# Four column groups for the weighted sums of a graph attention layer, with sums by ones

## The chip, the cores and the metric

The kernel runs on one core of a Trainium2 chip. The metric is the device time of one execution in microseconds (us); lower is better. The core's engines are named as in the profile: PE (TensorE matmul) with PEld (its weight loads), DVE (VectorE), ACT (ScalarE), POOL (GpSimd) and SP (SyncE, which here only issues DMAs). Each works through its own queue in order; they wait for one another by semaphores.

## The reference, cut to what matters

The whole computation is a stack of four graph layers over x of shape 128 x 128 x 128 (samples, tokens, features) with an integer adjacency of the same shape. Each layer normalizes its input, applies a relu, and adds its result to x. The change concerns layer 2, a graph attention with four heads of 32 features, and two helpers that it shares with layer 3, an attention with one head of 128 features.

```python
h = jnp.maximum(_layernorm(x, axis=-1), 0.0)
x = x + _L2_gnn_ref(h, adj, L2_gnn_W, L2_gnn_b, L2_gnn_a)

def _L2_gnn_ref(x, adj, W, b, a):
    H, D = 4, 32
    h = (x @ W + b).reshape(Bb, Nn, H, D)
    e_i = jnp.einsum('bnhd,d->bnh', h, a[:D, 0])
    e_j = jnp.einsum('bnhd,d->bnh', h, a[D:, 0])
    e = e_i[:, :, None, :] + e_j[:, None, :, :]
    e = jnp.where(e > 0, e, 0.2 * e)
    e = jnp.where(adj[..., None] > 0, e, NEG)
    attn = jax.nn.softmax(e, axis=2)
    out = jnp.einsum('bijh,bjhd->bihd', attn, h)
    return out.reshape(Bb, Nn, H * D)
```

Layer 3 has the same form with one head, and an elu on its result.

## The kernel before, in words

The kernel has three long stages: up to about 1500 us layer 0 and the pairwise differences of layer 1; up to about 2317 us the rest of layer 1, during which the DMA engines are busy; and then the last stage, layers 2 and 3. Only the last stage is edited. Samples are worked on in 32 groups of G = 4. `attention(g)` lists the work of one group as steps; every step has a name, an engine, a cost, the steps that it follows, the PSUM tiles that it takes and those that it gives back. `_planned` takes the lists of all groups, with a distance of PERIOD = 12 us between groups, and writes out one order for all engines from those costs; that order is then issued as it stands. Several groups are under way at once, so that each engine's queue mixes steps of different groups and layers. PSUM is shared as ONE = 4 tiles of one bank (tag "one") and TWO = 2 tiles of two banks (tag "two").

The steps of one group, for layer 2:

- `off` (L1190, POOL) makes a mask of missing edges from the stored bytes. `y`, `yl`, `po`, `x1` end layer 1 and give x.
- `layer(2, ...)` begins with `moments` (L1217, L1219, DVE) and `root` (L225, L226, L1223, L1224, POOL), which give the factor `rs` and offset `nb` of each token. `normed` (L1229) applies them with a relu, one sample at a time, on ACT. `turned` (L1235, PE) transposes, a copy to `hT` (L1304, ACT) follows, and `projected` (L1241, L1244, PE) multiplies by the layer's weights. The result `pr` holds the values and, in its last columns, both score vectors.
- `scores` (L1252, DVE) takes the scores out as `v`; `values` (L1257, L1258, POOL) presets the value tile `wr` and `values2` (L1267, ACT) copies the values in. In layer 2 a head has 33 columns: 32 values and a one, so that a product with `wr` also gives the softmax's sum.
- `split` (L1283, L1285, POOL) splits the scores into bf16 pieces, `crossed` (L1290, PE) transposes them, ACT copies `left` (L1312), and `right` (L1296, DVE) spreads the other factor over four parts with 0/1 masks, for each layer once.
- For each sample k: `summed` (L1332, L1335, PE) makes the scores of all four heads in one bank and masks them, for two samples at a time; `exps` (L1318, L1319, ACT) takes two exponentials; `higher` (L1322, DVE) takes the larger one as `e`, 128 x 4 x 128 with the neighbours on the partitions.
- `weighed` (L1345, PE) multiplies: for each head, `e` of that head is the stationary operand and a window of 128 columns of `wr` is the moving one. The first 33 columns of each result are values and sum. `scaled` (L1359, L1360, DVE) takes the reciprocal of the sums of two samples (128 x 8) and multiplies; after both pairs, `x2` (L1365, DVE) adds to x.

Layer 3 then runs the same steps with one head; its products are L1381 and its division L1385 and L1386. Three DVE steps and an exponential give the elu, and SP stores the group (L1400).

Of the kernel before, what the change touches and what calls it, by code (L numbers as in the profile page):

```python
# [9 lines left out]
F32 = mybir.dt.float32  # L10
I32 = mybir.dt.int32
BF16 = mybir.dt.bfloat16
U8 = mybir.dt.uint8
AF = mybir.ActivationFunctionType
OP = mybir.AluOpType
AX = mybir.AxisListType

P = 128
G = 4
# [20 lines left out]
ONE, TWO = 4, 2  # L40
# [128 lines left out]
def tile_gnn_stack(ctx: ExitStack, tc: tile.TileContext, a: dict, out: bass.AP):  # L169
    nc = tc.nc  # L170
# [18 lines left out]
    ident = const.tile([P, P], F32, name="ident")  # L189
# [3 lines left out]
    ones = const.tile([P, P], F32, name="ones")  # L193
# [23 lines left out]
    M8 = [res.tile([P, G, P], U8, tag=f"m{g}", name=f"m{g}") for g in range(NG)]  # L217
# [44 lines left out]
    with tc.tile_pool(name="c0", bufs=1) as c0, tc.tile_pool(name="p0", bufs=2) as p0, ExitStack() as ctx0:  # L262

        both = c0.tile([P, 2, P], F32, name="both")
# [280 lines left out]
        flat = a["adj"].rearrange("b t s -> b (t s)").rearrange("b (c n) -> c b n", c=PARTS)  # L545
# [100 lines left out]
        with tc.If(nc.values_load(flag, min_val=0, max_val=1) > 0) as cmp, \  # L646
# [6 lines left out]
            for g in range(NG):  # L653
                x = pr.tile([P, G, P], F32, name="x")
# [5 lines left out]
                hT = pr.tile([P, G, P], F32, name="hT")  # L660
# [3 lines left out]
                o = pr.tile([P, G, P], F32, name="o")  # L664
# [107 lines left out]
    with tc.tile_pool(name="bn", bufs=1) as bn:  # L772


        w_all, w_last, n = 2.0 * G * (KH - 1) * P, 1.0 * G * P, 1.0 * NB * P * P
        last = bn.tile([P, 1], F32, name="last")
# [16 lines left out]
        m = fold_sum(ST1[:, :, :, 0])  # L793
# [24 lines left out]
    with tc.tile_pool(name="c1", bufs=1, reuse_waits="tile") as c1, \  # L818
# [7 lines left out]
                         start=True, stop=True)  # L826
        own = c1.tile([P, 1], F32, name="own")
# [11 lines left out]
                         start=True, stop=True)  # L839
# [7 lines left out]
        for n in range(2):  # L847
            t = c1.tile([P, G, 1 + 2 * KH], F32, name=f"sk{n}")
# [296 lines left out]
    with tc.If(nc.values_load(bounded, min_val=0, max_val=1) > 0) as cmp, \  # L1145
# [10 lines left out]
        def attention(g):  # L1156


            t, steps = {}, []

            def step(name, engine, cost, after, work, takes=(), last=()):
                steps.append(((g, name), engine, cost, [(g, n) for n in after], takes, last, work))

            def sb(name, shape, dtype=F32):
                t[name] = p3.tile(shape, dtype, tag=name, bufs=BUFS[name], name=name)
                return t[name]

            def bank(name, shape=(P, G, P), dtype=F32):
                t[name] = ps3.tile(list(shape), dtype, tag="one", bufs=ONE, name=name)
                return t[name]  # L1170

            def two(name, n):

                t[name] = ps3.tile([P, 2, 512], F32, tag="two", bufs=TWO, name=name)
                t[name] = t[name][:, :, 0:2 * n].rearrange("p a (b c) -> p a b c", b=2)
                return t[name]
# [10 lines left out]
            lx = () if on_chip else ("lx",)  # L1187

            def masked():
                nc.gpsimd.tensor_scalar(sb("off", [P, G, P], BF16), M8[g], 0.0, None, op0=OP.is_equal)  # L1190

            step("off", "Pool", 1.5, lx, masked)
            step("y", "ACT", 0.75, () if on_chip else ("lz",), lambda: nc.scalar.activation(
                t["y"], t["y"], AF.Identity, bias=bias2, scale=scale2[:, 0:1]))
            step("yl", "DVE", 0.65, ("y",), lambda: nc.vector.scalar_tensor_tensor(
# [2 lines left out]
            def rest():  # L1198
                po = bank("po")
                for k in range(G):  # L1200
# [4 lines left out]
                 last=("po",))  # L1205

            def layer(n, heads, wx, first):

                q = lambda name: name + str(n)
                N = P + 2 * heads  # L1210
                mv, rs, nb = q("mv"), q("rs"), q("nb")
# [14 lines left out]
                def normed():  # L1226
                    h = sb("h", [P, G, P])
                    for k in range(G):
                        nc.scalar.activation(h[:, k, :], t["x"][:, k, :], AF.Relu, bias=t[nb][:, k:k + 1],  # L1229
                                             scale=t[rs][:, k:k + 1])  # L1230

                def turned():
                    pt = bank(q("pt"))
# [19 lines left out]

                def values():
                    if first:
                        wr = sb(q("wr"), [P, G + 1, 4, 33])
                        nc.gpsimd.memset(wr[:, 0:G, :, 32:33], 1.0)  # L1257
                        nc.gpsimd.memset(wr[:, G, 0:3, :], 0.0)  # L1258
                    else:
                        wr = sb(q("wr"), [P, G, 129])  # L1260
                        nc.gpsimd.memset(wr[:, :, P:], 1.0)

                def values2():
                    pr, wr = t[q("pr")], t[q("wr")]
                    for a in range(2):
                        if first:
                            nc.scalar.copy(wr[:, 2 * a:2 * a + 2, :, 0:32],  # L1267
                                           pr[:, a, :, 0:P].rearrange("p b (c d) -> p b c d", c=4))
                        else:
                            nc.scalar.copy(wr[:, 2 * a:2 * a + 2, 0:P], pr[:, a, :, 0:P])  # L1270
# [22 lines left out]
                rows, own = (32 * G, own_h) if first else (32, own_k)  # L1293

                def right():
                    nc.vector.tensor_tensor(sb(q("right"), [P, 4, P], BF16)[0:rows],  # L1296
                                            t[q("pe")][0:rows, 1:2, :].to_broadcast([rows, 4, P]),
                                            own[0:rows, :, None].to_broadcast([rows, 4, P]), OP.mult)

                step(mv, "DVE", 1.05, ("x1",) if first else ("x2",), moments)  # L1300
                step(rs, "Pool", 1.7, (mv,), root)
                step(q("h"), "ACT", 1.2, (rs,), normed)
                step(q("pt"), "PE", 0.5, (q("h"),), turned, takes=(q("pt"),))
                step(q("hT"), "ACT", 0.52, (q("pt"),), lambda: nc.scalar.copy(sb(q("hT"), [P, G, P]), t[q("pt")]),  # L1304
                     last=(q("pt"),))
                step(q("pr"), "PE", 1.0, (q("hT"),), projected, takes=("2" + q("pr"),))
                step(q("v"), "DVE", 0.3, (q("pr"),), scores)
                step(q("w1"), "Pool", 0.3, (q("h"),), values)
                step(q("wr"), "ACT", 0.65, (q("v"), q("w1")), values2, last=("2" + q("pr"),))
                step(q("sp"), "Pool", 1.2, (q("v"),), split)  # L1310
                step(q("pe"), "PE", 0.2, (q("sp"),), crossed, takes=(q("pe"),))
                step(q("left"), "ACT", 0.3, (q("pe"),), lambda: nc.scalar.copy(  # L1312
                    sb(q("left"), [P, P], BF16)[0:rows], t[q("pe")][0:rows, 0, :]))
                step(q("right"), "DVE", 0.6, (q("left"),), right, last=(q("pe"),))

            def exps(ps, e):

# [7 lines left out]
            for k in range(G):  # L1325
                ps, e, pv = f"ps{k}", f"e{k}", f"pv{k // 2}"

                def summed(k=k):

                    for j in (k, k + 1):  # L1330
                        r = slice(32 * j, 32 * j + 32)
                        nc.tensor.matmul(bank(f"ps{j}"), t["left2"][r, :], t["right2"][r, :, :], start=True,  # L1332
                                         stop=False, skip_group_check=True)
                    for j in (k, k + 1):
                        nc.tensor.matmul(t[f"ps{j}"], t["off"][:, j, :], no_edge[:, None, :].to_broadcast([P, 4, P]),  # L1335
                                         start=False, stop=True, skip_group_check=True)

                def weighed(k=k, e=e, pv=pv):

                    if k % 2 == 0:  # L1340
                        t[pv] = ps3.tile([P, 2, 4, P], F32, tag="two", bufs=TWO, name=pv)
                    flat = t["wr2"].rearrange("p k c d -> p (k c d)")
                    for hd in range(4):
                        at = 33 * (4 * k + hd)
                        nc.tensor.matmul(t[pv][:, k % 2, hd, :], t[e][:, hd, :], flat[:, at:at + P],  # L1345
                                         start=True, stop=True)

                if k % 2 == 0:
                    step(ps, "PE", 0.8, ("right2", "off"), summed, takes=(ps, f"ps{k + 1}"))
                step(e, "ACT", 1.05, (f"ps{k // 2 * 2}",), lambda ps=ps, e=e: exps(ps, e))  # L1350
                step(e + "m", "DVE", 0.62, (e,), lambda ps=ps, e=e: higher(ps, e), last=(ps,))
                step(f"w{k}", "PE", 0.95, (e + "m", "wr2") + ((f"w{k - 1}",) if k % 2 else ()), weighed,
                     takes=("2" + pv,) if k % 2 == 0 else ())
                if k % 2:
                    def scaled(k=k, pv=pv):
                        sums = sb("sums2", [P, 2, 4, 1])
                        if k == 1:
                            sb("o2", [P, G, P])
                        nc.vector.reciprocal(sums, t[pv][:, :, :, 32:33])  # L1359
                        nc.vector.tensor_tensor(t["o2"][:, k - 1:k + 1, :].rearrange("p k (a b) -> p k a b", a=4),  # L1360
                                                t[pv][:, :, :, 0:32], sums.to_broadcast([P, 2, 4, 32]), OP.mult)

                    step(f"o{k}", "DVE", 0.55, (f"w{k}",) + (("o1",) if k == 3 else ()), scaled, last=("2" + pv,))

            step("x2", "DVE", 0.62, ("o3",), lambda: nc.vector.scalar_tensor_tensor(  # L1365
                t["x"], t["o2"], -1.0, t["x"], op0=OP.add, op1=OP.add))

            layer(3, 1, w3x, False)

# [40 lines left out]
    with cmp.Else(), tc.tile_pool(name="c2", bufs=1) as c2, tc.tile_pool(name="p2", bufs=5) as p2, \  # L1410
# [25 lines left out]
        left = c2.tile([3, 4], F32, name="left")  # L1436
# [188 lines left out]
```

## Time and profile before

| | us |
|---|---|
| median of three runs | 2778.75 (2771.28 to 2781.27) |
| the profiled execution's own time | 2781.11 |
| its span | 2779.3 |
| first instruction of the last stage (L1193) | 2317.6 |
| PE, DVE, ACT, POOL busy over the span | 2457.4, 2472.0, 2388.7, 1724.0 |

The span runs from the profiled execution's first to its last instruction; the execution's own time has 1.8 us more around it. Busy time counts an engine as busy while at least one of its instructions runs. Instructions of one engine overlap by a little, so that the mean length of one times the count is more than the busy time. A matmul of f32 operands appears as two passes, each with its own weight load. Shapes are partitions x elements; "out<-in" are the program's names of the tiles. "Idle before" is the time for which the engine stood idle before instructions of that group, followed by what ended the wait.

### The profile page before, as it was taken

To read this page: it belongs to the slowest core of one execution; us is meant where nothing else is said; L and a number is where in the kernel's file an instruction comes from. 1 tells how busy PE (TensorE), PEld (TensorE's weight loads), DVE (VectorE), ACT (ScalarE), POOL (GpSimd) and SP (SyncE) were. 2 spreads that over 40 slices of the span, in tenths; PEclk is the share of its full clock that TensorE was granted. 3 is DMA by queue.
4 is the path that set the end of the run, shared out by engine and by line. 5 is a ranking of instruction groups with operands and counts; after the bars stand their busy time and mean duration, and the time that the engine had idled before them with its cause. 6 is when DMAs were issued, how large, how long until landed. Compare 5 with 4: busy or idle time off the path is not lost.

```text
span 2779.3 us, 42065 instructions
## 1 busy us (share of the span) xinstructions
PE 2457.4 (88%) x14521; PEld 1182.0 (43%) x14521; DVE 2472.0 (89%) x4712; ACT 2388.7 (86%) x2837; POOL 1724.0 (62%) x1629
## 2 busy tenths in 40 slices
PE   3899999999999999999998789888888897999896
PEld 2333333333333333333332344444444445777675
DVE  4899999999999999999999688888888887899976
ACT  4899999999999999999998778778778766899985
POOL 5799999999999999999997001111000115565642
PEclk7999999999999999999999899999999999999998
DMA  7455555555555555555543899999999971121110
GB/s 283 171 223 201 212 201 210 210 212 201 208 201 208 211 209 207 208 207 215 206 193 125 330 409 411 410 411 410 409 410 410 409 266 54 46 69 58 58 31 25
DMA packets 195933, 635.66 MB, mean 229 GB/s; under 512 B 32755, under 2 KB 100470, under 8 KB 132214
## 3 DMA queue, kind: packets, MB, share of 16 engines
q1 hardware_dynamic: 195264, 632.62, 58.6%
q8 instruction: 120, 1.97, 0.3%
q14 instruction: 111, 0.91, 0.1%
q10 hardware_dynamic: 438, 0.17, 0.0%
HBM read 328.84 MB, written 303.89 MB: 228 GB/s over the span
## 4 chain that ended last, share of the span: by engine, by line
ACT 33%; PE 22%; DVE 19%; issue 11%; DMA 10%; POOL 3%; SPq 1%; ACTq 0%; DVEq 0%; POOLq 0%
ACT d L360 11%; ACT z L336 11%; PE hp L322 6%; PE ps L871 5%; DMA rows<-sk 4%; DVE d L312 3%; DMA u<-rows 3%; DVE z L914 3%; DMA z<-hp 3%; PE hp L325 2%; ACT h L1229 2%; PE pk L878 2%; PE pv L1345 2%; ACT o L462 1%; ACT h L503 1%
## 5 line engine op out<-in xcount | busy, mean ns | idle before, releaser
L312 POOL TENSOR_TENSOR d<-xe 128x2048 f32<-128x2048 f32 x256 | 1074.1, 4202 | 67.1 <-PE hp L322 48.9
L322 PE MATMUL hp<-d,w1T 128*64 128x512 f32 x4096 | 999.4, 603 | 119.8 <-ACT z L336 96.8
L360 ACT ACTIVATE d<-d 128x2048 f32<-128x2048 f32 x384 | 734.6, 1935 | 24.7 <-POOL d L312 18.2
L312 DVE TENSOR_TENSOR d<-xe,xp 128x2048 f32<-128x2048 f32 x256 | 579.5, 2264 | 5.8 <-PE hp L322 3.1
L322 PEld LDWEIGHTS hp<-d,w1T 128*64 128x64 f32 x4096 | 286.2, 137 | 640.4 <-issue 466.6
L336 ACT COPY z<-hp 128x1024 f32<-128x1024 f32 x512 | 516.9, 1028 | 47.1 <-PE hp L325 24.4
L962 POOL TENSOR_TENSOR x<-x,bt 128x512 f32<-128x512 f32 x32 | 46.5, 1455 | 672.1 <-DMA x<-x 629.0
L350 DVE BATCH_NORM_STATS2 st<-z 128x6 f32<-128x512 f32 x512 | 349.3, 682 | 42.4 <-ACT z L336 42.1
L351 DVE BATCH_NORM_STATS2 st<-z 128x6 f32<-128x512 f32 (+1 forms) x512 | 329.3, 643 | 0.0
L914 DVE SCALAR_TENSOR_TENSOR z<-z 128x2048 f32<-128x2048 f32 x128 | 296.6, 2317 | 6.5 <-ACT z L896 6.5
L896 ACT ACTIVATE z<-z,bias,scale 128x2048 f32<-128x2048 f32 x128 | 267.1, 2087 | 9.3 <-DVE bias L809 7.7
L325 PE MATMUL hp<-both_t,xw 128*64 128x512 f32 x1024 | 268.3, 596 | 0.0
L900 ACT ACTIVATE zr<-z,bias,scale 128x2048 f32<-128x2048 f32 x128 | 267.3, 2088 | 0.9 <-DMA z<-hp 0.9
L871 PE MATMUL ps<-z,w2z 128*32 128x512 f32 x1024 | 144.7, 638 | 65.1 <-DVE z L914 64.9
L878 PEld LDWEIGHTS pk<-pick,su 128*128 128x128 f32 x1024 | 127.4, 196 | 136.2 <-DVE su L892 94.0
L878 PE MATMUL pk<-pick,su 128*128 128x16 f32 x1024 | 139.9, 269 | 19.9 <-DVE su L892 19.3
L1345 PE MATMUL pv<-wr,e 128*128 128x128 f32 x1024 | 141.7, 285 | 5.8 <-DVE e L1322 4.0
L871 PE MATMUL ps<-z,w2l 128*32 128x512 f32 x1024 | 142.7, 626 | 0.0
L871 PE MATMUL ps<-zr,w2r 128*32 128x512 f32 x1024 | 141.0, 623 | 0.0
L325 PEld LDWEIGHTS hp<-both_t,xw 128*64 128x64 f32 x1024 | 80.7, 138 | 140.7 <-issue 140.7
L1345 PEld LDWEIGHTS pv<-wr,e 128*128 128x128 f32 x1024 | 129.4, 197 | 13.5 <-DVE e L1322 4.1
L1322 DVE SCALAR_TENSOR_TENSOR e<-e,ps 128x512 f32<-128x512 f32 x160 | 106.8, 677 | 25.9 <-ACT ps L1319 25.1
(243 smaller groups left out, 3823.2 us busy)
## 6 DMA issues: line engine op xcount, KB each, us to landing
hp<-z SPq DMA_DIRECT2D x248, 1024.0 KB, 3.9
z<-hp SPq DMA_DIRECT2D x248, 1024.0 KB, 14.2
x<-x SPq DMA_DIRECT2D x118, 256.0 KB, 5.9
u<-rows SPq DMA_DIRECT2D x32, 384.0 KB, 11.6
x<-in_x_dram SPq DMA_DIRECT2D x32, 256.0 KB, 3.1
adj<-in_adj_dram SPq DMA_DIRECT2D x32, 256.0 KB, 3.5
part<-in_adj_dram SPq DMA_DIRECT2D x16, 512.0 KB, 7.6
out_dram<-x SPq DMA_DIRECT2D x32, 256.0 KB, 2.4
```

The lines of the kernel that those rows point to most:

```text
L312: eng.tensor_tensor(d, ahead, x[:, None, None, :].to_broadcast([P, 2, KC, P]), OP.max if t == BY_MAX else OP.subtract)
L322: nc.tensor.matmul(hp[64 * hh:64 * hh + 64, c:c + 512], w1T2 if by_max else w1T, d[:, hh, c:c + 512], start=True, stop=not by_max, skip_gr ...
L325: nc.tensor.matmul(hp[64 * hh:64 * hh + 64, c:c + 512], XW[i // NT // 2][:, i // NT % 2, :], both_t.rearrange("p h k i -> p h (k i)")[:, h ...
L336: nc.scalar.copy(half_of(b, t), linear.pop(i))
L350: nc.vector.bn_stats(st[:, 2 * t, :], hs[:, 0:512])
L351: nc.vector.bn_stats(st[:, 2 * t + 1, :], hs[:, 512:1024 - P * last])
L360: nc.scalar.activation(diffs[i], diffs[i], AF.Abs)
L871: nc.tensor.matmul(ps[32 * c:32 * c + 32, :], w[:, w0:w0 + 32], v[:, 512 * c:512 * c + 512], start=j0 == 0, stop=w is w2r, skip_group_chec ...
L878: nc.tensor.matmul(pk[:, kk, 0:16], su[:, kk, :], pick.rearrange("p h j -> p (h j)"), start=True, stop=True)
L900: nc.scalar.activation(zr, z1, AF.Relu, bias=bias1, scale=scale1[:, 0:1])
L914: nc.vector.scalar_tensor_tensor(z0, z0, 0.01, z0, op0=OP.mult, op1=OP.max)
L1345: nc.tensor.matmul(t[pv][:, k % 2, hd, :], t[e][:, hd, :], flat[:, at:at + P], start=True, stop=True)
```

## The change

Five edits, all in the last stage:

- In `weighed`, the operands change places: the 32 value columns of a head are stationary and `e` of that head, 128 columns, is moving. Head hd writes to partitions 32·hd to 32·hd + 31, so that the four heads use four column groups of PE's array. A second set of four products has 32 columns of ones as the stationary operand and gives the sums, repeated over the 32 partitions of a head. All four samples write into one two-bank tile `pv2`, values in its first bank, sums in its second.
- `scaled` runs once for a group, after the last sample: a reciprocal of 128 x 512 and a product of 128 x 512. Its result has features on the partitions, so `by_token` transposes it on PE into `ot`, and `x2` reads `ot`. The value tile has 32 columns for a head; its presets in layer 2 go.
- `normed` moves from ACT to POOL, without the relu; the copy to `hT` does the relu. This holds for both layers.
- `right` moves from DVE, one instruction, to ACT, four instructions, each with a mask as its per-partition scale. This too holds for both layers.
- `off` becomes a multiplication by -1 and an addition of 1 in place of a comparison with zero. The costs given to the planner follow, and its order with them.

```diff
             def masked():
-                nc.gpsimd.tensor_scalar(sb("off", [P, G, P], BF16), M8[g], 0.0, None, op0=OP.is_equal)
+                nc.gpsimd.tensor_scalar(sb("off", [P, G, P], BF16), M8[g], -1.0, 1.0, op0=OP.mult, op1=OP.add)
-            step("off", "Pool", 1.5, lx, masked)
+            step("off", "Pool", 0.7, lx, masked)
...
                     for k in range(G):
-                        nc.scalar.activation(h[:, k, :], t["x"][:, k, :], AF.Relu, bias=t[nb][:, k:k + 1],
-                                             scale=t[rs][:, k:k + 1])
+                        nc.gpsimd.tensor_scalar(h[:, k, :], t["x"][:, k, :], t[rs][:, k:k + 1], t[nb][:, k:k + 1],
+                                                op0=OP.mult, op1=OP.add)
...
                     if first:
-                        wr = sb(q("wr"), [P, G + 1, 4, 33])
-                        nc.gpsimd.memset(wr[:, 0:G, :, 32:33], 1.0)
-                        nc.gpsimd.memset(wr[:, G, 0:3, :], 0.0)
+                        sb(q("wr"), [P, G, 4, 32])
...
                 def right():
-                    nc.vector.tensor_tensor(sb(q("right"), [P, 4, P], BF16)[0:rows],
-                                            t[q("pe")][0:rows, 1:2, :].to_broadcast([rows, 4, P]),
-                                            own[0:rows, :, None].to_broadcast([rows, 4, P]), OP.mult)
+                    to = sb(q("right"), [P, 4, P], BF16)
+                    for part in range(4):
+                        nc.scalar.activation(to[0:rows, part, :], t[q("pe")][0:rows, 1, :], AF.Identity,
+                                             scale=own[0:rows, part:part + 1])
...
-                step(q("h"), "ACT", 1.2, (rs,), normed)
+                step(q("h"), "Pool", 1.85, (rs,), normed)
-                step(q("hT"), "ACT", 0.52, (q("pt"),), lambda: nc.scalar.copy(sb(q("hT"), [P, G, P]), t[q("pt")]),
+                step(q("hT"), "ACT", 0.52, (q("pt"),), lambda: nc.scalar.activation(
+                    sb(q("hT"), [P, G, P]), t[q("pt")], AF.Relu),
                      last=(q("pt"),))
-                step(q("right"), "DVE", 0.6, (q("left"),), right, last=(q("pe"),))
+                step(q("right"), "ACT", 0.95, (q("left"),), right, last=(q("pe"),))
...
-                    flat = t["wr2"].rearrange("p k c d -> p (k c d)")
-                    for hd in range(4):
-                        at = 33 * (4 * k + hd)
-                        nc.tensor.matmul(t[pv][:, k % 2, hd, :], t[e][:, hd, :], flat[:, at:at + P],
-                                         start=True, stop=True)
+                    if k == 0:
+                        two("pv2", 256)
+                    for n, left in enumerate((t["wr2"][:, k], ones.rearrange("p (a b) -> p a b", a=4))):
+                        for hd in range(4):
+                            nc.tensor.matmul(t["pv2"][32 * hd:32 * hd + 32, n, k // 2, P * (k % 2):P * (k % 2 + 1)],
+                                             left[:, hd, :], t[e][:, hd, :], start=True, stop=True,
+                                             skip_group_check=True)
...
-                        nc.vector.reciprocal(sums, t[pv][:, :, :, 32:33])
-                        nc.vector.tensor_tensor(t["o2"][:, k - 1:k + 1, :].rearrange("p k (a b) -> p k a b", a=4),
-                                                t[pv][:, :, :, 0:32], sums.to_broadcast([P, 2, 4, 32]), OP.mult)
-                    step(f"o{k}", "DVE", 0.55, (f"w{k}",) + (("o1",) if k == 3 else ()), scaled, last=("2" + pv,))
-            step("x2", "DVE", 0.62, ("o3",), lambda: nc.vector.scalar_tensor_tensor(
-                t["x"], t["o2"], -1.0, t["x"], op0=OP.add, op1=OP.add))
+            def scaled():
+                sums, o = sb("sums2", [P, G, P]), sb("o2", [P, G, P])
+                both = t["pv2"].rearrange("p n a b -> p n (a b)")
+                nc.vector.reciprocal(sums.rearrange("p k c -> p (k c)"), both[:, 1, :])
+                nc.vector.tensor_tensor(o.rearrange("p k c -> p (k c)"), both[:, 0, :],
+                                        sums.rearrange("p k c -> p (k c)"), OP.mult)
+            def by_token():
+                to = bank("ot")
+                for k in range(G):
+                    nc.tensor.transpose(to[:, k, :], t["o2"][:, k, :], ident)
+            step("o2", "DVE", 1.3, ("w3",), scaled, last=("2pv2",))
+            step("ot", "PE", 0.6, ("o2",), by_token, takes=("ot",))
+            step("x2", "DVE", 0.62, ("ot",), lambda: nc.vector.scalar_tensor_tensor(
+                t["x"], t["ot"], -1.0, t["x"], op0=OP.add, op1=OP.add), last=("ot",))
```

More of the change, by code (lines that the diff above doesn't have):

```diff
@@ L1266, in values2 @@
                         if first:
-                            nc.scalar.copy(wr[:, 2 * a:2 * a + 2, :, 0:32],
+                            nc.scalar.copy(wr[:, 2 * a:2 * a + 2, :, :],
                                            pr[:, a, :, 0:P].rearrange("p b (c d) -> p b c d", c=4))
@@ L1307, in layer @@
                 step(q("v"), "DVE", 0.3, (q("pr"),), scores)
-                step(q("w1"), "Pool", 0.3, (q("h"),), values)
+                step(q("w1"), "Pool", 0.0 if first else 0.15, (q("h"),), values)
                 step(q("wr"), "ACT", 0.65, (q("v"), q("w1")), values2, last=("2" + q("pr"),))
@@ L1336, in summed, with weighed @@
                                          start=False, stop=True, skip_group_check=True)
-                def weighed(k=k, e=e, pv=pv):
-                    if k % 2 == 0:
-                        t[pv] = ps3.tile([P, 2, 4, P], F32, tag="two", bufs=TWO, name=pv)
-                    flat = t["wr2"].rearrange("p k c d -> p (k c d)")
-                    for hd in range(4):
-                        at = 33 * (4 * k + hd)
-                        nc.tensor.matmul(t[pv][:, k % 2, hd, :], t[e][:, hd, :], flat[:, at:at + P],
-                                         start=True, stop=True)
+                def weighed(k=k, e=e):
+                    if k == 0:
[5 more added lines that the diff above has]
+                                             skip_group_check=True)
                 if k % 2 == 0:
@@ L1351, in attention @@
                 step(e + "m", "DVE", 0.62, (e,), lambda ps=ps, e=e: higher(ps, e), last=(ps,))
[L1352 to L1360, printed above, removed]
-                                                t[pv][:, :, :, 0:32], sums.to_broadcast([P, 2, 4, 32]), OP.mult)
-                    step(f"o{k}", "DVE", 0.55, (f"w{k}",) + (("o1",) if k == 3 else ()), scaled, last=("2" + pv,))
-            step("x2", "DVE", 0.62, ("o3",), lambda: nc.vector.scalar_tensor_tensor(
-                t["x"], t["o2"], -1.0, t["x"], op0=OP.add, op1=OP.add))
+                step(f"w{k}", "PE", 0.6, (e + "m", "wr2") + ((f"w{k - 1}",) if k else ()), weighed,
+                     takes=("2pv2",) if k == 0 else ())
+            def scaled():
[12 more added lines that the diff above has]
+                t["x"], t["ot"], -1.0, t["x"], op0=OP.add, op1=OP.add), last=("ot",))
             layer(3, 1, w3x, False)
```

## The prediction

> **What bounds the kernel now.** I read the page's share of busy time first, then its slices, where DMA falls from nine tenths to one or two for the last seven slices: that is the stage the change touches, and nothing before it is edited. The table by windows gives that stage (first line, from its first instruction to the end) and its steady part (second line, from the fourth output store at 2415.4 us to the twenty-eighth at 2738.9 us, 24 groups of four samples). Columns: stretch, length, then busy us of each engine with its instructions.
>
> ```profile
> core 0: us, PE busy (x) PEld busy (x) DVE busy (x) ACT busy (x) POOL busy (x), PEclk, DMA share, GB/s
> 2317.00:2780.00 463.00, 402.19 (x2912) 320.69 (x2912) 381.11 (x1219) 382.62 (x896) 252.71 (x712) 0.94 0.15 45
> 2415.40:2738.90 323.50, 294.18 (x2188) 236.65 (x2187) 278.27 (x884) 280.31 (x658) 173.00 (x501) 0.97 0.17 52
> ```
>
> The steady stage costs 323.5 / 24 = 13.5 us a group. Over 32 groups the whole stage keeps PE 12.57, DVE 11.91, ACT 11.96 and POOL 7.9 us busy per group. Three engines are level and together set the pace; DVE idles 81 us of the 462 us from 2317 to the end. So an engine that is relieved brings little while the other two stay, and an engine that gets 2 us more sets the end alone. What the edits concern is in the groups kept apart by shape (count | busy us, mean ns | idle before):
>
> ```profile
> L1322 DVE SCALAR_TENSOR_TENSOR e<-e,ps 128x512 f32<-128x512 f32 x160 | 106.8, 677 | 25.9 <-ACT ps L1319 25.1
> L1360 DVE TENSOR_TENSOR o<-pv,sums 128x256 f32<-128x256 f32 x64 | 27.2, 424 | 2.2
> L1386 DVE TENSOR_TENSOR o<-pv,sums 128x512 f32<-128x512 f32 x32 | 22.1, 691 | 1.1
> L1296 DVE TENSOR_TENSOR right<-pe,own_h 128x512 bf16<-128x512 bf16 x32 | 21.6, 682 | 2.1 <-ACT left L1312 2.1
> L1296 DVE TENSOR_TENSOR right<-pe,own_k 32x512 bf16<-32x512 bf16 x32 | 21.4, 668 | 0.5 <-ACT left L1312 0.5
> L1359 DVE RECIPROCAL sums<-pv 128x8 f32<-128x8 f32 x64 | 12.6, 197 | 15.8 <-PE pv L1345 15.8
> L1252 DVE COPY v<-pr 128x16 f32<-128x16 f32 x64 | 7.7, 163 | 3.9 <-PE pr L1244 3.7
> L1252 DVE COPY v<-pr 128x4 f32<-128x4 f32 x64 | 7.2, 155 | 5.9 <-PE pr L1244 5.5 <-PE pe L1290 0.2
> L1385 DVE RECIPROCAL sums<-pv 128x4 f32<-128x4 f32 x32 | 5.4, 170 | 12.3 <-PE pv L1381 12.3
> ```
>
> The small rows matter most. A copy of 16 columns takes 8 ns more than one of 4, under 1 ns a column. A reciprocal of 8 columns takes 27 ns more than one of 4: **about 6.75 ns a column**. Today only 2 x 8 + 4 columns a group pass through it.
>
> ```profile
> L1345 PE MATMUL pv<-wr,e 128*128 128x128 f32 x1024 | 141.7, 285 | 5.8 <-DVE e L1322 4.0 <-ACT wr L1267 1.4 <-DVE o L1360 0.2
> L1229 ACT ACTIVATE h<-x,nb,rs 128x128 f32<-128x128 f32 x256 | 105.4, 491 | 26.9 <-POOL nb L1224 12.8 <-POOL wr L1261 8.0 <-DVE st L1217 4.3
> L1312 ACT COPY left<-pe 128x128 bf16<-128x128 bf16 x32 | 8.8, 282 | 2.3 <-PE pe L1290 2.3
> L1312 ACT COPY left<-pe 32x128 bf16<-32x128 bf16 x32 | 8.0, 249 | 4.3 <-PE pe L1290 4.2
> ```
>
> Here 1024 matmuls are 32 a group: each f32 product is two passes. Last, the timeline of TensorE in the stage before this one, where four column groups are already in use:
>
> ```profile
> 1898.82 0.27 PE L940 MATMUL pt<-ident,u 128*128 128x128 f32 x1
> 1899.03 1.06 PE L871 MATMUL ps<-z,w2z 128*32 128x512 f32 x8
> 1899.91 1.04 PE L871 MATMUL ps<-z,w2l 128*32 128x512 f32 x8
> ```
>
> Eight 512-column passes end in 1.06 us, two rounds of four, 0.43 us a round: the groups run at once. The step from 128-column to 32-column tiles cost 0.20 us from start to start, where transposes in a row follow each other every 0.11 us.
>
> [...]
>
> **The change, per group.**
>
> *Sums by ones.* The stationary ones repeat every softmax sum over a head's 32 rows, so the sums fill 128 x 512, and the two reciprocals of 8 columns become one of 512. On DVE two reciprocals (0.23 us from start to start) and two products (0.42, less 0.08 of overlap) go: -1.14 us. One 512-column product from PSUM comes: 0.69 - 0.08 = +0.61. The reciprocal is the unknown. From below: [...]as for L1386, 0.7 us. From the row's slope: 0.14 + 512 x 6.75 ns = 3.6. [...]I take 4.4: with 0.14 fixed it gives 173 and 207 ns for 4 and 8 columns, against 170 and 197 on average.
>
> *Right factors to ScalarE.* DVE loses two of 0.59 us pitch: -1.18 (in the timeline `right` starts at 2521.53 us and its follower at 2522.12). ACT gains eight activations, a PSUM copy of that size plus one pointer: about 375 ns, 282 ns apart: +2.26.
>
> *Norms to GpSimd.* ACT loses eight h of about 0.39 (four last 1.65 us in the timeline): -3.15, so ACT goes to 11.96 - 3.15 + 2.26 = 11.1. The relu rides on the copy of hT at no cost. POOL gains eight one-input 128x128 steps; between the 0.27 of its 128x4 steps (L225) and an estimate of 0.5 I take 0.4: +3.2. The mask as multiply and add costs 0.62 at its fastest elsewhere (median 0.94) instead of 1.53: -0.6 to -0.9. The memsets of wr save 0.3. POOL: about 10, still not the bound, even at 0.5 a step. Its two h's stand ahead of other groups' splits in its queue, so left and right come later; PE's tuned slack of several groups in flight covers that, and if not, up to 1 us a group is in my upper end.
>
> *Products.* PE drops 32 passes of 0.112 = 3.58 us. It gains, per k, four rounds of four passes of 128 columns, each round a quarter of 0.43 = 0.107, plus one mode change in and one out (0.09 each) and a weight load laid bare (0.1): 0.72, or 2.9 for four. Four transposes add 0.44. Net -0.3: PE about 12.3. From above, with no concurrency, 64 x 0.11 = 7.0.
>
> *DVE in sum*: 11.91 - 1.14 + 0.61 - 1.18 + 4.4 = **14.6 us**, 2.7 more than now and 2.3 above PE. Over 32 groups, 467 us against 381.
>
> *Waits.* Today half of the values come free after two small operations; now one two-bank tile is held from the first product until reciprocal and product are through, 5.1 us, one of the two such tiles. In the changed order of instructions PE reaches the transposes `ot` in one steady group after transposing a split, projecting values twice and transposing an h, some 2.9 us: PE then stands about 2 us, and behind `ot` are the next products and scores. On DVE itself, the scores' splits (`v`), maxima (`e`) and the moments of other groups queue behind the reciprocal; GpSimd already waited 41.3 us for `v` in 2400 to 2700 us. SP only has stores later; its loads are long done. In the tail the last group passes reciprocal, transposes and two `right` steps alone: about +5 us.
>
> *Sum.* DVE is now clearly ahead of the others, so it starves less on average, but PE's stand at `ot` and the tail give it back. I keep 75 of its 81 us idle: 467 + 75 = 542 us for the stage against 462, **+80 us**. The profiled execution took 2781.1 us (span 2779.3 and 1.8 around it), so 2861; the median of the runs, 2778.75, is 2.4 lower: 2859. With 3.6 for the reciprocal DVE's work is 441: +54, 2833. Idle between 50 and 110 us gives +55 to +115.
>
> **Rivals.**
> *The reciprocal is cheap* (0.7 us, 1.3 ns a column). Then DVE is 10.9, ACT 11.1, PE 12.3: the stage gains 0.3 to 0.9 us a group, less a longer tail: 2750 to 2775, say 2765. For it speaks only that 27 ns is a small difference of short instructions; against it, 64 and 32 of them and the copies beside them. It decides below about 1.7 us for 512 columns, where DVE comes back to 11.9.
> *PE's stand at `ot` grows*: both engines wait for each other in turn, 17.5 to 18 us a group: 2910 to 2930. Against it: several groups are in flight.
> *The column groups do not overlap at 128 columns* (the change does not do what it says): PE 12.57 + 3.4 + 0.44 = 16.4 us, DVE hidden behind it: about 2910. Against it, the lines at 1899 us.
>
> **How the numbers follow.** DVE bound by the reciprocal 0.75, growing stand 0.12, no overlap 0.05, cheap reciprocal 0.08 (of which 0.02 within 0.5%, some 14 us, about what a measurement of this kernel can tell from no change). The range 2822 to 2900 holds the main case with both its reciprocal prices and idle bounds, and the lower edge of the standing PE.
>
> **What would show it.** A row of 128x512 reciprocals at about 4.4 us (right), under 1.7 us (the main step is wrong); DVE over 90% busy in the steady part with PE and ACT under 80%; `right` near 0.37 us, h on POOL near 0.4; the first passes of four heads starting within some 10 ns of each other; PE's wait at `ot` put down to DVE's product.

## Result, and the profile after

The changed kernel takes 2851.58 us, median of four runs (2848.05 to 2852.57), against 2778.03 us for the kernel before on the same chip: 1.0268 times its time, 95% interval 1.0256 to 1.0281. The profiled execution took 2852.57 us with a span of 2850.8. The prediction was 2859. The last stage alone grew: from its first instruction to the end 461.7 us before and 536.6 after.

The table by windows of the changed kernel, whole last stage and steady part (fourth to twenty-eighth output store); columns as before, PEclk being the granted TensorE clock as a share of full speed:

```profile
core 0: us, PE busy (x) PEld busy (x) DVE busy (x) ACT busy (x) POOL busy (x), PEclk, DMA share, GB/s
2314.17:2850.80 536.63, 411.70 (x4064) 284.73 (x4064) 435.00 (x1088) 354.49 (x896) 332.44 (x902) 0.88 0.13 39
2424.20:2810.00 385.80, 304.02 (x3061) 210.50 (x3061) 321.91 (x790) 265.83 (x678) 238.60 (x656) 0.88 0.14 44
```

A group now costs 385.8 / 24 = 16.1 us. Divided by 32, the stage keeps PE 12.9, DVE 13.6, ACT 11.1 and POOL 10.4 us busy. DVE now stands at the top, 0.7 us above PE, with ACT well below. But in the steady part DVE is busy for only 83% of the time (321.91 / 385.80), PE for 79% and ACT for 69%, and PE's mean granted clock is 0.88 where it was 0.97. Both matter below.

The groups that answer to those shown of before:

```profile
L1229 POOL TENSOR_SCALAR h<-x,rs,nb 128x128 f32<-128x128 f32 x256 | 117.9, 474 | 1.4
L1358 DVE RECIPROCAL sums<-pv 128x512 f32<-128x512 f32 x32 | 107.3, 3352 | 15.7 <-PE pv L1344 15.6
L1322 DVE SCALAR_TENSOR_TENSOR e<-e,ps 128x512 f32<-128x512 f32 x160 | 105.8, 677 | 20.2 <-ACT ps L1319 19.9
...
L1344 PE MATMUL pv<-e,wr 128*32 128x128 f32 x1024 | 60.5, 305 | 17.7 <-DVE e L1322 11.9 <-DVE o L1359 2.8 <-DVE v L1252 2.4
L1344 PE MATMUL pv<-e,ones 128*32 128x128 f32 x1024 | 58.2, 296 | 0.0
...
L1244 PE MATMUL pr<-w3x,hT 128*128 128x130 f32 x256 | 42.7, 320 | 14.5 <-DVE o L1359 8.4 <-DVE v L1252 2.1 <-ACT ps L1319 1.6
...
L1296 ACT ACTIVATE right<-pe,own_h 128x128 bf16<-128x128 bf16 x128 | 36.5, 380 | 0.0
...
L1296 ACT ACTIVATE right<-pe,own_k 32x128 bf16<-32x128 bf16 x128 | 35.0, 343 | 0.0
...
L1365 PE MATMUL ot<-ident,o 128*128 128x128 f32 x128 | 26.4, 343 | 29.3 <-DVE o L1359 21.2 <-DVE sums L1389 4.0 <-ACT hT L1303 2.0
...
L1359 DVE TENSOR_TENSOR o<-pv,sums 128x512 f32<-128x512 f32 x32 | 22.1, 691 | 1.1
...
L1190 POOL TENSOR_SCALAR off<-m 128x512 bf16<-128x512 uint8 x32 | 21.7, 684 | 0.1
...
L1241 PE MATMUL pr<-b_parts,ones 3*128 3x272 bf16 x64 | 13.7, 297 | 7.0 <-DVE o L1359 6.9
```

One instruction a group, the reciprocal, takes 3.35 us and 107 us in all, as much as all 160 maxima of the scores. The row of `ot` shows PE idle for 29.3 us ahead of the new transposes, 21.2 of them until DVE's product ended. The same product ends another 18.1 us of PE's idle time, ahead of `pr` (8.4 and 6.9) and of the weighted sums (2.8): these write to two-bank tiles, and `pv2` is one of the two.

The timeline of DVE and PE of the changed kernel around one such division:

```profile
2561.50 3.35 DVE L1358 RECIPROCAL sums<-pv 128x512 f32<-128x512 f32 x1
2564.89 0.69 DVE L1359 TENSOR_TENSOR o<-pv,sums 128x512 f32<-128x512 f32 x1
...
2568.48 0.65 DVE L1322 SCALAR_TENSOR_TENSOR e<-e,ps 128x512 f32<-128x512 f32 x1
2571.81 0.26 DVE L1252 COPY v<-pr 128x16 f32<-128x16 f32 x2 [2.68 <-PE pr L1244]
2574.00 0.69 DVE L1322 SCALAR_TENSOR_TENSOR e<-e,ps 128x512 f32<-128x512 f32 x1 [1.94 <-ACT ps L1319]
```

```profile
2563.36 0.40 PE L1379 MATMUL ps<-no_edge,off 128*128 128x128 bf16 x4
2565.72 0.62 PE L1365 MATMUL ot<-ident,o 128*128 128x128 f32 x4 [1.97 <-ACT hT L1303]
...
2567.12 1.97 PE L1235 MATMUL pt<-ident,h 128*128 128x128 f32 x8
2569.03 0.63 PE L1241 MATMUL pr<-b_parts,ones 3*128 3x272 bf16 x2
2569.59 2.18 PE L1244 MATMUL pr<-w2x,hT 128*128 128x136 f32 x8
...
2587.13 1.19 PE L1244 MATMUL pr<-w2x,hT 128*128 128x136 f32 x8
```

`ot` is next in PE's queue and waits for DVE's product, which ends at 2565.58, 0.14 us before `ot` starts; PE stands 1.97 us. (The trace names `hT`, but the transposes read the product.) From 2567 on PE works at about half pace: eight passes over 136 columns last 2.18 us, where the same eight last 1.19 at 2587. Behind that, DVE waits 2.68 us for `pr` and 1.94 us for exponentials of scores that PE made late. The windows of the same stretch, again of the changed kernel, give the clock:

```profile
2560.00:2564.00 4.00, 2.81 (x43) 1.63 (x43) 3.83 (x4) 4.00 (x14) 3.56 (x9) 1.00 0.51 136
2564.00:2567.00 3.00, 1.28 (x20) 0.88 (x20) 2.97 (x5) 1.73 (x5) 0.00 (x0) 0.92 0.21 81
2567.00:2573.50 6.50, 6.50 (x28) 3.90 (x24) 2.35 (x12) 2.46 (x6) 2.79 (x9) 0.51 0.01 3
```

The granted clock is 1.00, 0.92 and then 0.51. After 3.00 us in which PE was busy for 1.28 it works for 6.5 us at half speed, and DVE's two waits fall into that time. PE did not stand all through: in the 3.4 us before the fall at 2566.5 us (the length of the shortest stretch at half clock in the trace's record) it was still busy for 1.43 us.

The fall is one of many. The trace's record of the clock has 22 falls to half in the changed kernel's last stage and 8 in that of the kernel before, and in the 3.4 us ahead of each of them PE was busy for at most 2.0 us. Cut into windows of 1 us, the changed stage has 128 at half clock (PEclk under 0.7), which hold 53 of DVE's 102 us of idle time; before, there were 50, with 25 of 81 us. This says when DVE is idle, not how long it would be idle at full clock.

### The profile page after: what moved, and what is told of

Same layout as the page of the kernel before. It is cut to its first block, busy times and chain, and to the rows that moved or that the text cites. A ratio compares the mean times of both kernels' runs of the same rounds, so it can differ in the third digit from the quotient of the medians.

```text
span 2850.8 us, 44433 instructions
## 1 busy us (share of the span) xinstructions
PE 2456.7 (86%) x15673; PEld 1144.0 (40%) x15673; DVE 2524.7 (89%) x4584; ACT 2360.4 (83%) x2837; POOL 1818.0 (64%) x1821
## 4 chain that ended last, share of the span: by engine, by line
ACT 27%; DVE 21%; PE 20%; DMA 14%; issue 11%; POOL 4%; SPq 1%; ACTq 0%; DVEq 0%; POOLq 0%
ACT z L336 10%; ACT d L360 10%; PE hp L322 5%; DMA z<-hp 5%; DMA rows<-sk 5%; DMA u<-rows 4%; DVE d L312 4%; DVE sums L1358 4%; PE ps L871 4%; PE hp L325 2%; DVE z L914 2%; DVE st L350 1%; PE pv L1344 1%; ACT o L462 1%; PE pk L878 1%
## 5 line engine op out<-in xcount | busy, mean ns | idle before, releaser
L1358 DVE RECIPROCAL sums<-pv 128x512 f32<-128x512 f32 x32 | 107.3, 3352 | 15.7 <-PE pv L1344 15.6
L1229 POOL TENSOR_SCALAR h<-x,rs,nb 128x128 f32<-128x128 f32 x256 | 117.9, 474 | 1.4
```

## Experiments

Two theories stood at the start. **T**: the wide reciprocal is the cost; VectorE's own work sets the time. **W**: the new chain (one held tile, a transposition, another order) makes TensorE stand, whatever the division takes. A third, **M**, put part of the loss on the moved norms and right factors. Stage length and engine times below come from the table by windows of each kernel, from its first `y` activation to its end; idle is stage length less DVE's busy time.

| kernel | median us | stage | DVE busy | DVE idle | ACT busy | PEclk |
|---|---|---|---|---|---|---|
| before | 2778.0 | 461.7 | 380.7 | 81 | 382.6 | 0.94 |
| changed | 2851.6 | 536.6 | 435.0 | 102 | 354.5 | 0.88 |
| e1_copy | 2772.5 | 454.1 | 350.9 | 103 | 351.5 | 0.92 |
| e2_twice | 2987.6 | 671.9 | 544.1 | 128 | 354.6 | 0.77 |
| e3_moves | 2785.7 | 467.1 | 349.5 | 118 | 352.7 | 0.95 |
| e4_products | 2897.8 | 580.7 | 470.9 | 110 | 388.0 | 0.83 |
| e5_period | 2854.7 | 546.4 | 435.9 | 110 | 356.4 | 0.84 |
| e5_cost | 2830.2 | 516.0 | 432.2 | 84 | 354.8 | 0.89 |
| e6_parts | 2853.4 | 540.2 | 435.1 | 105 | 354.2 | 0.87 |
| e7_own_steps | 2839.1 | 524.2 | 432.0 | 92 | 357.3 | 0.88 |
| e8_mask | 2778.3 | 462.3 | 381.5 | 81 | 382.2 | 0.95 |
| e9_mask_norms | 2786.7 | 470.6 | 384.7 | 86 | 293.3 | 0.94 |
| e10_h_on_act | 2878.2 | 564.4 | 435.8 | 129 | 447.9 | 0.84 |
| e11_right_on_dve | 2872.4 | 548.8 | 470.4 | 78 | 293.4 | 0.87 |

The stage is that of each kernel's one profiled execution, which can lie off its median (that of e11_right_on_dve is 8 us shorter, that of e5_period 5 us longer); the kernel before, run beside them, had medians of 2775.8 to 2778.0.

### The price of the division: none, once, twice

```diff
 # e1_copy
-                nc.vector.reciprocal(sums.rearrange("p k c -> p (k c)"), both[:, 1, :])
+                nc.vector.tensor_copy(sums.rearrange("p k c -> p (k c)"), both[:, 1, :])
 # e2_twice
                 nc.vector.reciprocal(sums.rearrange("p k c -> p (k c)"), both[:, 1, :])
+                nc.vector.reciprocal(sums.rearrange("p k c -> p (k c)"), both[:, 1, :])
```

e1_copy:

> The changed kernel with the 128x512 reciprocal of the sums replaced by a copy of the same shape from PSUM: the division of layer 2 is left out, every other instruction and the order stay. Theory T (the reciprocal's 3.35 us on VectorE is the cost): VectorE falls by 2.7 us a group to about 10.9, below TensorE, and the time comes back to 2765 to 2790. Rival W (the long chain: one held tile, the transposes and the later order stall TensorE whatever the division costs): the time stays above 2815.

e2_twice:

> The changed kernel with the reciprocal issued twice into the same tile. Theory T: VectorE is the bound and its idle time stays about 100 us, so 32 x 3.3 us come on top nearly in full: 2940 to 2965. Rival W (VectorE has slack at 83% busy and the stall is elsewhere): less than 60 us on top, below 2910.

Groups by shape of e1_copy; columns as above:

```profile
L1358 DVE COPY sums<-pv 128x512 f32<-128x512 f32 x32 | 21.9, 684 | 19.8 <-PE pv L1344 19.5
...
L1365 PE MATMUL ot<-ident,o 128*128 128x128 f32 x128 | 20.6, 286 | 3.2 <-DVE e L1322 2.1 <-ACT right L1296 0.6 <-DVE o L1359 0.5
```

The copy takes 0.68 us in place of 3.35, PE's stand ahead of `ot` falls from 29.3 to 3.2 us, and the whole loss is gone: 2772.47 us, 0.9981 of the kernel before (0.9971 to 0.9991). The chain, the tile and the transposes are all still there, so W falls as a cause on its own. With the reciprocal twice, DVE is busy 109 us longer and the time rises by 136, beyond T's range: the second one adds its work and 26 us of idle time, and PE's mean clock falls to 0.77. T holds as to the cause. From the copy to one division the time rises by 79 us for 84 us of DVE's work; the second division costs more than its own length.

The falls of the clock follow the division: 9 without it, 22 with it, 37 with it twice. Both runs change DVE's work and the wait for it together; how much is the wait is seen below, where the order changes.

### The moves, taken alone and taken back

```diff
 # e3_moves: the kernel before, with
+                nc.gpsimd.tensor_scalar(sb("off", [P, G, P], BF16), M8[g], -1.0, 1.0, op0=OP.mult, op1=OP.add)
+                step(q("h"), "Pool", 1.85, (rs,), normed)      # tensor_scalar on GpSimd; relu in hT
+                step(q("right"), "ACT", 0.95, (q("left"),), right, last=(q("pe"),))
 # e8_mask: the first line only; e9_mask_norms: the first two
 # e4_products: the changed kernel, its order kept, all three issued as in the kernel before
 # e10_h_on_act: the norms alone issued on ACT; e11_right_on_dve: the right factors alone on DVE
```

e3_moves:

> The kernel before with only the mask's arithmetic, the norms on GpSimd and the right factors on ScalarE; the products and the division stay as before. Theory T: nothing here costs VectorE, which loses 1.2 us a group, ScalarE about 0.9; TensorE's 12.6 us a group stay: 2750 to 2780. Rival M (the moves lengthen each group's chain through GpSimd and ScalarE, and that is part of the loss): over 2795.

e4_products:

> The changed kernel in the same order of steps, but with mask, norms and right factors issued as before (comparison, ScalarE, VectorE); the new products, sums and the division stay. Theory T: VectorE gets 1.2 us a group back, to 14.8: 2875 to 2895. Rival M: the moves were the cost, so taking them back gains: below 2840.

e8_mask:

> The kernel before with the mask by multiply and add alone (GpSimd 0.85 us a group less), the products, norms and right factors as before. If GpSimd's queue, where the mask stands ahead of the roots and splits, is part of the stage's length: 2762 to 2772, a candidate for a version faster than both. If its idle time covers it: within 5 us of the kernel before.

e9_mask_norms:

> The kernel before with the mask's arithmetic and the norms on GpSimd, right factors left on VectorE. ScalarE loses 3.15 us a group, VectorE and TensorE keep their work. If ScalarE's queue shares in the bound: 2755 to 2770, a candidate for a version faster than both. If TensorE's 12.6 us and each group's chain, now through a norm of 1.9 us on GpSimd, set the pace: 2775 to 2792.

e10_h_on_act:

> The changed kernel in the same order, with the norms alone issued on ScalarE as before. VectorE's work stays, ScalarE goes from 11.1 to about 14.3 us a group, GpSimd from 10.4 to 6.7. Under a VectorE bound with 102 us of idle time: 2845 to 2865; if ScalarE, now above VectorE's 13.6, takes over: 2865 to 2900.

e11_right_on_dve:

> The changed kernel in the same order, with the right factors alone issued on VectorE as before. VectorE gets 1.2 us a group back, 38 us in all: 2880 to 2900 if VectorE's work is what counts, as much as all three moves together taken back (2897.75). Below 2865 if ScalarE's eight steps cost the chain as much as they spare VectorE.

In the kernel before, the moves gain nothing. All three give 2785.73 us, 1.0029 (1.0020 to 1.0038); mask and norms 1.0040 (1.0027 to 1.0053); the mask alone 1.0006 (0.9999 to 1.0014). For the last two this is the second case of what was expected: relieving GpSimd or ScalarE alone brought nothing. In e3_moves DVE and ACT each have about 30 us less to do, and idle longer instead. The table by windows of e3_moves:

```profile
2311.39:2778.50 467.11, 402.82 (x2912) 318.17 (x2912) 349.47 (x1152) 352.70 (x896) 349.93 (x966) 0.95 0.15 45
```

PE's 402.8 us are those of the kernel before (402.2), and GpSimd's have gone from 252 to 350. I had set 2750 to 2780 as T's range, too low, and M's bound of 2795 was not reached either: PE's work and the longer chain through GpSimd stay. Which of the two holds the stage was not separated.

In the changed kernel the same moves do pay. Taken back together they cost 46 us, 3 us beyond T's range; norms alone 27, right factors alone 21. Moving the right factors back puts 35 us on DVE, of which 21 appear: less than the first case of e11_right_on_dve, more than the second. Moving the norms back leaves DVE at 435.8 us and lifts ACT to 447.9, and the time lies in the range of the second case; that ACT then sets the pace is argued, since ACT too is idle for 117 us of that stage. So M falls as a cause: taking the moves back does not gain. How much they soften the loss is less sure. These three runs keep an order that was written for the moved steps, and part of the 46 us may come from work that no longer fits its order.

### The order, and the block in DVE's queue

```diff
 # e5_period
-PERIOD, FIRST, HOP, LANDING = 12, 5, 0.2, 3.0
+PERIOD, FIRST, HOP, LANDING = 13, 5, 0.2, 3.0
 # e5_cost: also
-            step("o2", "DVE", 1.3, ("w3",), scaled, last=("2pv2",))
+            step("o2", "DVE", 3.9, ("w3",), scaled, last=("2pv2",))
 # e6_parts: in scaled, for k in range(G)
+                    nc.vector.reciprocal(sums[:, k, :], both[:, 1, P * k:P * k + P])
 # e7_own_steps: distance 13, the reciprocal of sample k as a step of its own
+                step(f"r{k}", "DVE", 0.95, (f"w{k}",), inverted)
+            step("o2", "DVE", 0.65, ("r0", "r1", "r2", "r3"), scaled, last=("2pv2",))
```

e5_period:

> The changed kernel with the planner's distance between groups 13 in place of 12; nothing else. It is the control of the next two, which need 13. All theories: within 10 us of the changed kernel, 2842 to 2862.

e5_cost:

> The changed kernel with distance 13 and the planner's cost of the division set to 3.9 us, near what the trace shows (3.35 + 0.69 less overlap), in place of 1.3. Theory O (the order written for a 1.3 us division makes TensorE and the others stand; VectorE's idle time of 102 us holds it): 2815 to 2835, below the control by 15 or more. Theory D (the idle time comes with the long division itself, whatever the order): within 12 us of the control.

e6_parts:

> The changed kernel with the reciprocal in four instructions of 128 columns, one after another in the same step. If the price is 0.14 us and 6.3 ns a column, each takes about 0.95 us, 3.5 us together with overlap against 3.35, and the time rises by 3 to 10 us to about 2858 (theories O and D both). Nothing waits less, since the product follows all four. If a reciprocal had a price that grows otherwise with its width, the row shows it.

e7_own_steps:

> The changed kernel with distance 13 and the four reciprocals of 128 columns as steps of their own (cost 0.95 to the planner), each placed after its sample's products; the product of 512 columns follows the last. VectorE's work is 0.2 us a group more than in the control. Theory D, in the form that the uninterrupted block and the wait after the last product are what hurts: only 0.95 + 0.69 us follow the last product, idle falls by 25 us or more, 2815 to 2835. If idle time has other causes: 2850 to 2870.

The distance alone does little (2854.69). Telling the planner what the division costs brings 24.5 us against that control, to 2830.16, within O's range: DVE's idle time goes from 110 to 84 us with 4 us less of busy time. So the order written for a division of 1.3 us is worth about a third of the loss. The rows of `ot` in e5_period and then in e5_cost show where the wait went:

```profile
L1365 PE MATMUL ot<-ident,o 128*128 128x128 f32 x128 | 27.9, 358 | 33.7 <-DVE o L1359 17.3 <-DVE e L1322 14.4 <-DVE v L1252 2.0
L1365 PE MATMUL ot<-ident,o 128*128 128x128 f32 x128 | 25.5, 336 | 4.2 <-DVE e L1322 2.2 <-DVE o L1359 2.0
```

PE's stand ahead of `ot` is nearly gone, and 2830 us is still 54 above the kernel before. As steps of their own the four reciprocals bring 15.6 us, and DVE waits 47 us ahead of them for PE's products. Idle time falls by 18 us, where theory D asked for 25 or more, and 2839.11 lies in neither of the two ranges. Both gains are mostly idle time given back; neither is enough, since the work remains. The group of the pieces in e6_parts:

```profile
L1359 DVE RECIPROCAL sums<-pv 128x128 f32<-128x128 f32 x128 | 108.3, 907 | 15.8 <-PE pv L1344 15.6
```

Four pieces of 0.91 us keep DVE 108.3 us busy, as long as the whole ones (107.3), and the time is the same to 2 us, where a rise of 3 to 10 was expected. Widths of 4, 8, 128 and 512 columns took 0.17, 0.20, 0.91 and 3.35 us: 6.4 ns a column between the last two.

No version here beats the kernel before by more than the 0.2% of e1_copy, which does not divide. Against e3_moves, which has the same three moves and the old products, e1_copy is 13 us faster. So the column groups themselves may be worth something where the division is cheap; no run with a cheap division that still divides, or with an order written for it, was made.

## Why the prediction was right, and where it was lucky

- **The main case** is what happened: the sums by ones send 512 columns through the reciprocal, DVE becomes the bound, the median rises by 74 us where 80 were forecast. e1_copy and e2_twice show the cause by taking it away and doubling it. The signs asked for were met in part: PE and ACT are under 80% busy in the steady part, but DVE is not over 90%.
- **The price of the reciprocal was mis-sized.** I took 4.4 us, an estimate of mine taken from no row of the trace; it is 3.35. The trace's own slope, 6.75 ns a column, comes nearer (3.6), though it rested on 27 ns. 1.05 us too much in 32 groups is 34 us.
- **The other terms of DVE's sum** fit: 467 us forecast, less those 34, is 433; measured 435.0.
- **The idle time was mis-sized the other way.** I kept 75 of 81 us, expecting DVE to starve less; it was 102, though the forecast asked for over 90% busy in the steady part and got 83%. The two errors, -34 and +27 us, nearly cancel. With the price from the slope, the text had +54 for the stage (2833), below the 2851.6 measured. So that the forecast came within 8 us is luck in part. The stated range was also narrower than it said: the slope's price with 50 us of idle time gives 491 us for the stage, +29, about 2808, which is below 2822.
- **What the idle term missed** was partly named: PE's stand at `ot`, costed at 2 us a group, is there, 1.97 us in the stretch shown and 29.3 / 32 = 0.9 us on average, and e5_cost shows that the order carries 24.5 us. The wait for the held two-bank tile, 18.1 us in all by the trace's account, was named but not costed, and the 5.1 us given for it count only the division and the product, not the four samples' sums before them. It was not seen that PE then works on at half clock. That this lower clock adds to DVE's idle time is read from the stretch at 2567 us, from the windows of 1 us and from the clocks in the table; no run held the clock up to show it alone.
- **ScalarE**: 11.1 us a group forecast, 354.5 / 32 = 11.1 measured, but by two errors that cancel. Without the norms ACT has 2.8 to 2.9 us less a group (e9_mask_norms against e8_mask, the changed kernel against e10_h_on_act) where 3.15 were forecast; the right factors add 1.9 (the changed kernel against e11_right_on_dve), not 2.26. One `right` takes 0.38 and 0.34 us against about 0.375, and 0.29 and 0.27 us apiece in busy time (36.5 and 35.0 us / 128) against 0.282; `left`, a copy of the same shapes without the scale, takes 0.27 and 0.25. The copy to `hT` takes 0.60 us with the relu and took 0.59 without it. **GpSimd**: about 10 forecast, 10.4 measured, h at 0.47 instead of the 0.4 taken between 0.27 and 0.5, the mask 0.68 instead of 0.62. **PE**: 12.3 forecast, 12.9 measured, at the lower clock; e1_copy has 12.0.
- **Products**: the first passes of the four heads start at 2544.737, 2544.743, 2544.750 and 2544.757 us, each some 7 ns after the one before and 20 ns from first to last, where about 10 ns were asked for. In the next lines, from the timeline of the changed kernel at full clock, the first product starts at 2544.74 us and the work after the sums at 2545.31: 0.57 us, of which four rounds are 0.44 and the step from 32-column back to 128-column tiles most of the rest (`po` starts 0.22 us after the last round, where rounds follow each other in 0.11). The first product starts 0.20 us after the last transpose, where transposes follow each other in 0.11. With these 0.09 us for the step to 32-column tiles, a sample costs 0.67 us against the 0.72 forecast. Of the rivals, the missing overlap is excluded by these rows and the cheap reciprocal by its own row (3.35 us); the growing stand happened in small.

```profile
2544.15 0.66 PE L1235 MATMUL pt<-ident,h 128*128 128x128 f32 x4
2544.74 0.42 PE L1344 MATMUL pv<-e,wr 128*32 128x128 f32 x8
2544.98 0.40 PE L1344 MATMUL pv<-e,ones 128*32 128x128 f32 x8
2545.31 1.16 PE L1201 MATMUL po<-wtyT,y 128*128 128x128 f32 x8
```

## What to carry to other kernels

Before a small operation is spread over a whole tile, compare two widths of it in the trace: here a slope of 6.4 ns a column made 512 columns cost more than everything that was saved around them. Where an order is written out from costs, a wrong cost can be paid twice, once as work and once in the waits of the engines placed behind it. Relieving an engine gave nothing while level ones stayed: the same moves cost 9 us in the kernel before, and taking them back cost the changed one 46 in its own order.

## What the runs showed of the hardware

A VectorE reciprocal costs about 6.4 ns a column more between 128 columns (0.91 us) and 512 (3.35 us), and cutting it into four pieces saves nothing (108.3 us against 107.3); this is about six times the slope of a copy (0.68 us for 512 columns, 0.16 for 4). After 3.4 us in which TensorE was busy for 1.43, its granted clock fell to half (0.51 over the next 6.5 us shown), and eight passes that take 1.19 us took 2.18. The last stage had 8 such falls before the change, 22 after it, 37 with the reciprocal twice and 9 with a copy in its place; its mean clock was 0.94, 0.88, 0.77 and 0.92. So here a longer instruction on one engine went with a lower clock on another: from the copy to the reciprocal PE's stand ahead of `ot` grew from 3.2 to 29.3 us and the mean clock went from 0.92 to 0.88. That the stand brings the falls is read from their order in time; no run shows it alone.
